# More query blocks beside the layer, a depthwise chunk moved to VectorE, and maxima spread by transposes one step after their fold

## The chip, the core and the metric

The kernel runs on one core of a Trainium2 chip. The metric is the device time of one execution in microseconds (us). The kernel before takes 5365.54 us, the median of three runs (5365.16 to 5367.03). All data are fp32.

## What is computed

The input x has four images of 64 x 64 tokens with 256 channels. Two layers follow each other.

```python
# layer 0: a gated block of scan and depthwise convolution, then a feed-forward
xz = layernorm(x) @ in_proj_W                 # 256 -> 2 * 384
x_proj, z = xz[..., :384], xz[..., 384:]
y_ssm = 0.5 * (scan_fwd(windows2x2(x_proj)) + scan_bwd(windows2x2(x_proj)))   # 8 states, 4 steps
y_dw = depthwise_conv3x3(x_proj)
y_conv = gelu(y_dw @ pw_W)
alpha = sigmoid(gate)
y = alpha * y_ssm + (1 - alpha) * y_conv
x1 = x + (y * silu(z)) @ out_W
x1 = x1 + gelu(layernorm(x1) @ fuse_W1 + b1) @ fuse_W2 + b2
# layer 1: attention over the 4096 tokens of each image
f, g, h = x1 @ Wf + bf, x1 @ Wg + bg, x1 @ Wh + bh     # 32, 32 and 256 wide
out = gamma * (softmax(g @ f.T) @ h @ Wo + bo) + x1
```

Both layers must give all their values; the output is `out`, of the shape of x.

## The kernel before, in words

**The first layer** goes in 32 layer blocks of 512 tokens (eight image rows), eight to an image. `first_layer` (L734) is a Python generator: each piece of it issues some instructions and then yields a number, its cost. For every layer block it runs `scan` (L413), which goes through 8 states times 3 time steps in both directions, in 48 scan steps: TensorE turns a decay tile into a PSUM bank (`turned`, L449), VectorE multiplies it with the state (`decayed`, L457 and L461), adds to the output (`given`, L467) and makes the next state (`carried`, L476). Between these pieces, `side` (L703) is fed in by credit (SHARE, 1.2): the depthwise convolution `conv` (L588) of the block before, its gate, its `tail` (L602) and the next block's `head` (L302). After the scan, `merge` (L547) turns the scan's output back to channels and adds it to xc, the projected input.

`depthwise` (L558) works on three chunks of 128 channels. Its argument `dense` says how many go over TensorE, as nine matmuls with diagonal weights (L565) and a copy on ACT (L571); each other chunk is nine operations on VectorE, L580 for the first tap and L582 for eight more. On the first image `dense` is 2, on the others 1. `tail` multiplies by pw_W (L613), takes Gelu on ACT (L618), scales by 1 - alpha on ACT (L625), adds alpha/2 times the merged scan on VectorE (L628), multiplies by the gate (L631), and goes on through out_W (L638), the feed-forward (L658, L669) and the values and keys of layer 1, which are written to memory.

**The attention** starts when the first image has left layer 0. An *early query block* is 128 queries of one image against its 4096 tokens. `weights` (L819) is a generator that makes the exponentials of the next block: scores on TensorE (L832), copies on ACT (L840), their maximum over tokens on VectorE (L846, L848, folded at L851), which is then made one number per query and spread over the partitions: two transposes (L854), a reduction (L856), a broadcast copy (L858), a matmul with the identity (L860), a copy on ACT (L862). Then for each of four tiles VectorE adds the negative maximum (L866) and ACT takes the exponential (L867). `attend` (L1013) multiplies the exponentials of the present block with the values (L1027), in eight steps of four value matmuls (512 tokens) each; after each step it takes one piece of `weights` of the next block and then calls `fill(RATE)` (L872), which takes pieces of the first layer until their costs make up RATE, 7.2. So RATE sets how much of the layer is issued beside one query block. `until` (L882) holds a new image's attention back until its layer blocks are done.

When the layer has ended, the rest of the attention goes by *late query blocks* of 256 queries (`late_weights` L912, `attend_late` L991), with the value matmuls on L1005 and the same spreading of maxima over L947 to L961.

**The order of work.** Every engine runs its instructions in one order, which the program's order of issue sets, with a scheduler that may move an instruction of a later piece ahead where the priorities allow it. TensorE's PSUM has three banks for the scan (`bank`), four for everything aside (`aside`, q0 to q3), and one for an accumulator (`pso`). SyncE's queue carries the loads of values (`vt`), queries, rests and the results.

The lines that pace the two are these:

```python
        for k in range(NI):
...
            next(beside, None)
            fill(RATE)
```

Of the kernel before, what the change touches and what calls it, by code (L numbers as in the profile page):

```python
# [22 lines left out]
AF = mybir.ActivationFunctionType  # L23
ALU = mybir.AluOpType
# [4 lines left out]
P = 128  # L29
# [11 lines left out]
CK = DIM // 8  # L41
EPS = 1e-5
SHARE = 1.2
RATE = 7.2


_VECS = [
# [12 lines left out]
def block_then_attention_kernel(  # L60
# [486 lines left out]
    def merge(at):  # L547

        y = merged.pop(at)
        xc = heads[at][1]  # L550
        for f in range(KI):
            py = bank()
            for t in range(4):
                nc.tensor.transpose(py[:, t * P : (t + 1) * P], y[:, t, f * P : (f + 1) * P], ident)
            nc.vector.scalar_tensor_tensor(xc[:, f, :], xc[:, f, :], dsum[:, f : f + 1], py, ALU.mult, ALU.add)
            yield 1.1

    def depthwise(ydw, dense):  # L558

# [28 lines left out]
    def conv(at):  # L588
        b = at // NBLK
        ydw = one.tile([P, KI, TOK], F32, tag="ff", name="ydw")  # L590
        ydws[at] = ydw
        yield from depthwise(ydw, KI - 1 if b == 0 else 1)

    def next_head(at):

# [6 lines left out]
    def tail(at):  # L602
# [7 lines left out]
        for f in range(KI):  # L610
# [10 lines left out]
                    AF.Gelu,  # L621
                )
            yield 2.58
        for f in range(KI):
            nc.scalar.activation(yz[:, f, :], yz[:, f, :], AF.Copy, scale=one_a[:, f : f + 1])  # L625

        for f in range(KI):
            nc.vector.scalar_tensor_tensor(  # L628
                yz[:, f, :], s[:, f, :], half_a[:, f : f + 1], yz[:, f, :], ALU.mult, ALU.add
            )  # L630
            nc.vector.tensor_tensor(yz[:, f, :], yz[:, f, :], zs[:, f, :], ALU.mult)  # L631
            yield 1.3
# [186 lines left out]
    def weights(b, q, es):  # L819


        fQ, gq = quarters[b], gqs.pop((b, q))
        mx = one.tile([P, TOK], F32, tag="mx", name="mx")
        for g in range(2):
            pr = four()

            with tc.high_priority():
                last = None
                for s in range(4):
                    at = g * TOK + s * P  # L830
                    for r in range(4):
                        ins = nc.tensor.matmul(  # L832
                            pr[r][:, s * P : (s + 1) * P], lhsT=fQ[CK * r : CK * (r + 1), at : at + P],
                            rhs=gq[CK * r : CK * (r + 1), :], start=True, stop=True,
                        )
                        last = behind(ins, last)
            for a in range(2):
                e = ep.tile([P, 2, TOK], F32, tag="eq", name="eq")
                for j in range(2):
                    nc.scalar.copy(e[:, j, :], pr[2 * a + j])  # L840
                es.append(e)
            yield
            for r in range(4):
                e = es[2 * g + r // 2]
                if g == 0 and r == 0:
                    nc.vector.tensor_tensor(mx, e[:, 0, :], e[:, 1, :], ALU.max)  # L846
                elif g == 1 or r > 1:
                    nc.vector.tensor_tensor(mx, mx, e[:, r % 2, :], ALU.max)  # L848
            if g == 0:
                yield  # L850
        nc.vector.tensor_tensor(mx[:, :QB], mx[:, :QB], mx[:, QB:], ALU.max)  # L851
        pm = aside()
        for c in range(2):
            nc.tensor.transpose(pm[:, c * P : (c + 1) * P], mx[:, c * P : (c + 1) * P], ident)  # L854
        nm = st.tile([P, 1], F32, tag="nm", name="nm")
        nc.vector.tensor_reduce(nm, pm[:, :QB], AX.X, ALU.max, negate=True)  # L856
        nmb = two.tile([P, P], F32, tag="nb", name="nmb")
        nc.vector.tensor_copy(nmb, nm.to_broadcast([P, P]))  # L858
        pn = aside()
        nc.tensor.matmul(pn[:, :P], lhsT=nmb, rhs=ident, start=True, stop=True)  # L860
        nb = two.tile([P, P], F32, tag="nb", name="nb")
        nc.scalar.copy(nb, pn[:, :P])  # L862
        yield
        for n, e in enumerate(es):
            e8 = e.rearrange("p r (s q) -> p (r s) q", s=4)
            nc.vector.tensor_tensor(e8, e8, nb.unsqueeze(1).broadcast_to([P, 8, P]), ALU.add)  # L866
            nc.scalar.activation(e, e, AF.Exp)  # L867
            yield
# [43 lines left out]
    def late_weights(b, q, odd, es):  # L912


        if b not in quarters:
            quarter(b, one, "norm" if b % 2 else "xo")
        fQ, gq = quarters[b], gqs.pop((b, q))
        mx = two.tile([P, 2, QB], F32, tag="uT", name="mx")
        for g in range(4):
            pr = four()  # L920
            for s in range(2):
                at = (g // 2) * TOK + (2 * (g % 2) + s) * P
                for r in range(4):
                    nc.tensor.matmul(  # L924
                        pr[r][:, s * QB : (s + 1) * QB], lhsT=fQ[CK * r : CK * (r + 1), at : at + P],
                        rhs=gq[CK * r : CK * (r + 1), :], start=True, stop=True,
                    )
            for a in range(2):
                pool, tag = SLOTS[8 * odd + 2 * g + a]
                e = pool.tile([P, 2, 2, QB], F32, tag=tag, name="eT")  # L930
                for j in range(2):
                    nc.scalar.copy(e[:, j], pr[2 * a + j].rearrange("p (s q) -> p s q", s=2))  # L932
                if g == 0 and a == 0:
                    nc.vector.tensor_tensor(mx, e[:, 0], e[:, 1], ALU.max)
                else:
                    for j in range(2):
                        nc.vector.tensor_tensor(mx, mx, e[:, j], ALU.max)  # L937
                es.append(e)
                yield
        yield  # L940
        yield
        both = one.tile([P, 2, QB], F32, tag="mx", name="m2")
        m2, nb = both[:, 0, :], both[:, 1, :]
        nc.vector.tensor_tensor(m2, mx[:, 0, :], mx[:, 1, :], ALU.max)
        pm = aside()
        for c in range(2):
            nc.tensor.transpose(pm[:, c * P : (c + 1) * P], m2[:, c * P : (c + 1) * P], ident)  # L947
        nm = st.tile([P, 2], F32, tag="nm", name="nm")
        nc.vector.tensor_reduce(
            nm, pm[:, :QB].rearrange("p (c k) -> p c k", c=2), AX.X, ALU.max, negate=True  # L950
        )
        wide = three.tile([P, 2, P], F32, tag="p", name="nmb")
        for c in range(2):
            nc.vector.tensor_copy(wide[:, c, :], nm[:, c : c + 1].to_broadcast([P, P]))
        yield
        pn = aside()
        for c in range(2):
            nc.tensor.matmul(
                pn[:, c * P : (c + 1) * P], lhsT=wide[:, c, :], rhs=ident, start=True, stop=True
            )  # L960
        nc.scalar.copy(nb, pn[:, :QB])  # L961
        for n, e in enumerate(es):
            e4 = e.rearrange("p r s q -> p (r s) q")
            nc.vector.tensor_tensor(e4, e4, nb.unsqueeze(1).broadcast_to([P, 4, QB]), ALU.add)  # L964
            nc.scalar.activation(e, e, AF.Exp)
            if n % 2:
                yield
# [42 lines left out]
                next(beside, None)  # L1010
        outcome(b, 2 * q, res, sums)

    def attend(b, q, es, beside, following):  # L1013

        res = load_rest(b, q, two, "res", 1)
        acc = pso.tile([P, TOK], F32, tag="pso", name="acc")
        for k in range(NI):
            for h in range(2):
                n = 2 * k + h
                if n + 4 < 2 * NI:  # L1020
                    load_values(b, q, n + 4)
                else:
                    following(n + 4 - 2 * NI)
                vt = vts.pop((b, q, n))
                for s in range(2):
                    a = (2 * h + s) * P
                    nc.tensor.matmul(  # L1027
                        acc[:, : DIM + 1], lhsT=es[k // 2][:, k % 2, a : a + P], rhs=vt[:, s, :],
                        start=(n == 0 and s == 0), stop=(n == 2 * NI - 1 and s == 1),
                    )  # L1030
            next(beside, None)
            fill(RATE)
        outcome(b, q, res, [acc])
# [17 lines left out]
    for n in range(4):  # L1051
        load_values(0, 0, n)
    es = []
    for _ in weights(0, 0, es):
        fill(RATE)
    a = 0
    while True:
# [6 lines left out]
        if late:  # L1064
            n0 = (b1, q1 // 2)
            load_late_queries(*n0)
            beside = twice(late_weights(*n0, 0, ahead))
            attend(b, q, es, beside, lambda n: load_late_values(*n0, n))
            es = ahead
            break  # L1070
        if q1 == 0:
            quarter(b1, one, "fQ")
        load_queries(b1, q1)
        attend(b, q, es, weights(b1, q1, ahead), lambda n: load_values(b1, q1, n))
        es = ahead
        a += 1
    odd, block = 0, n0
    while block:
# [98 lines left out]
```

## Time and profile before

| | value |
|---|---|
| median of three runs | 5365.54 us |
| the profiled execution, its time | 5371.37 us |
| its span, first to last instruction | 5369.6 us |
| mean granted TensorE clock | 0.978 |
| TensorE busy over the span | 5029.3 us (94%) |
| VectorE busy | 4558.3 us (85%) |
| ScalarE (ACT) busy | 3599.4 us (67%) |
| early query blocks (128 queries) | 76 |
| late query blocks (256 queries) | 26 |
| layer blocks | 32, of which 23 scans lie beside attention |

A row of a group reads: line, engine, operation, output <- inputs, size, count, then busy time in us and the mean duration of one in ns, then the idle time of the engine ahead of it and who ended it. A row of the chain of waits or the timeline reads: start in us, length in us, engine, line, tile, count. PE is TensorE's matmuls, PEld its weight loads, DVE VectorE, ACT ScalarE, POOL GpSimd, SP SyncE. A matmul of fp32 appears as two records.

The page's slices show the stages: the DMA row stands at 0 to 1 tenths while only the layer runs, at 3 while attention runs beside it, and at 5 in late attention.

### The profile page before, as it was taken

What the parts mean: (1) busy time and instruction counts of PE and PEld (TensorE: products, weight loads), DVE (VectorE), ACT (ScalarE), POOL (GpSimd) and SP (SyncE); (2) the same over time, 40 slices, a digit from 0 to 9 for tenths busy, and PEclk for the clock granted to TensorE, in tenths of its full rate; (3) what the DMA queues carried; (4) which work ended last, traced back from release to release, by engine and by line L of the source; (5) the groups of instructions that cost most, each with busy time, mean ns of one, the idle gap of its engine ahead of it and who ended that gap; (6) DMA issues with size and microseconds to landing.
All of it is one profiled execution on the core that took longest, in us unless ns stands there. A gap on an engine that the chain in (4) does not pass through costs nothing. (4 is left out here: it accounts for less than half of the span.)

```text
span 5369.6 us, 77772 instructions
## 1 busy us (share of the span) xinstructions
PE 5029.3 (94%) x27476; PEld 3585.9 (67%) x27476; DVE 4558.3 (85%) x8386; ACT 3599.4 (67%) x5530; POOL 206.0 (4%) x304
## 2 busy tenths in 40 slices
PE   7999999999999999999999999999999999999999
PEld 4555555666666666666666666666666667888887
DVE  7999999889988899889889998888998875666665
ACT  5767767778777677767777766767777744555554
POOL 0000000000000000000000000000000000000000
PEclk8999999999999999999999999999999999999999
DMA  1001001333333333333333333333343335555554
GB/s 47 26 30 31 19 25 31 98 109 107 115 113 112 114 112 114 118 115 107 111 116 111 115 116 107 114 114 113 102 123 113 110 116 165 146 146 146 146 146 138
DMA packets 333126, 558.45 MB, mean 104 GB/s; under 512 B 51904, under 2 KB 86976, under 8 KB 332736
## 3 DMA queue, kind: packets, MB, share of 16 engines
q1 hardware_dynamic: 330160, 551.52, 35.1%
q8 instruction: 217, 3.56, 0.3%
q10 hardware_dynamic: 2576, 1.97, 0.1%
q14 instruction: 173, 1.42, 0.1%
HBM read 494.49 MB, written 58.79 MB: 103 GB/s over the span
## 5 line engine op out<-in xcount | busy, mean ns | idle before, releaser
L1027 PE MATMUL acc<-vt,eq 128*128 128x257 f32 x4864 | 1234.2, 389 | 16.9 <-DVE res L975 13.0
L392 ACT ACTIVATE e<-dt,a_sc 128x384 f32<-128x384 f32 x1536 | 852.7, 611 | 347.0 <-PE bank L449 318.9
L1027 PEld LDWEIGHTS acc<-vt,eq 128*128 128x128 f32 x4864 | 891.1, 193 | 249.2 <-issue 116.6
L467 DVE SCALAR_TENSOR_TENSOR y<-p,bc,y 128x384 f32<-128x384 f32 x1536 | 948.8, 618 | 0.7
L449 PEld LDWEIGHTS bank<-ident,e 128*128 128x128 f32 x4320 | 524.3, 143 | 302.1 <-issue 125.7
L449 PE MATMUL bank<-ident,e 128*128 128x128 f32 x4320 | 647.8, 280 | 72.2 <-DVE p L461 29.3
L1005 PE MATMUL bank<-vt,eT 128*128 128x257 f32 x2496 | 625.8, 382 | 0.0
L476 DVE SCALAR_TENSOR_TENSOR h<-u,bc,p 128x384 f32<-128x384 f32 x1024 | 618.2, 621 | 0.1
L461 DVE TENSOR_TENSOR p<-bank,h 128x384 f32<-128x384 f32 x960 | 517.0, 552 | 52.4 <-PE bank L449 50.4
L1005 PEld LDWEIGHTS bank<-vt,eT 128*128 128x128 f32 x2496 | 467.1, 190 | 81.0 <-issue 12.9
L840 ACT COPY eq<-q 128x512 f32<-128x512 f32 x608 | 310.8, 593 | 179.7 <-PE q L832 166.4
L866 DVE TENSOR_TENSOR eq<-eq,nb 128x1024 f32<-128x1024 f32 x304 | 367.7, 1231 | 19.2 <-ACT nb L862 18.9
L867 ACT ACTIVATE eq<-eq 128x1024 f32<-128x1024 f32 x304 | 317.5, 1054 | 92.7 <-DVE eq L866 88.7
L937 DVE TENSOR_TENSOR mx<-mx,eT 128x512 f32<-128x512 f32 x364 | 252.0, 692 | 143.0 <-ACT eT L932 113.2
L848 DVE TENSOR_TENSOR mx<-mx,eq 128x512 f32<-128x512 f32 x456 | 317.0, 695 | 50.5 <-ACT eq L840 38.5
L932 ACT COPY eT<-q 128x512 f32<-128x512 f32 x416 | 213.2, 597 | 188.5 <-PE q L924 188.5
L392 ACT ACT_TABLE_LOAD x254 | 325.9, 1283 | 11.0 <-PE bank L449 6.8
L457 DVE SCALAR_TENSOR_TENSOR p<-bank,bc,u 128x384 f32<-128x384 f32 x480 | 294.1, 613 | 45.8 <-PE bank L449 45.6
L582 DVE SCALAR_TENSOR_TENSOR ydw<-xp,vec,ydw 128x512 f32<-128x512 f32 x448 | 325.4, 750 | 2.2
L613 PE MATMUL q<-ydw,wpw 128*128 128x512 f32 x576 | 269.3, 599 | 18.8 <-ACT eq L840 18.8
L964 DVE TENSOR_TENSOR eT<-eT,m 128x1024 f32<-128x1024 f32 x208 | 238.5, 1221 | 46.6 <-ACT m L961 46.6
L565 PE MATMUL q<-xp,dw 128*128 128x512 f32 x576 | 274.0, 597 | 2.4 <-ACT eq L840 2.4
(151 smaller groups left out, 7394.7 us busy)
## 6 DMA issues: line engine op xcount, KB each, us to landing
vt<-vod SPq DMA_DIRECT2D x1632, 257.0 KB, 2.8
vod<-vst SPq DMA_DIRECT2D x32, 514.0 KB, 4.4
xo<-in_x_dram SPq DMA_DIRECT2D x256, 64.0 KB, 2.7
xt<-in_x_dram SPq DMA_DIRECT2D x256, 64.0 KB, 1.9
x1d<-xo SPq DMA_DIRECT2D x32, 512.0 KB, 2.9
res<-x1d SPq DMA_DIRECT2D x76, 128.0 KB, 2.6
out_dram<-res SPq DMA_DIRECT2D x304, 32.0 KB, 1.6
fgd<-fg SPq DMA_DIRECT2D x32, 256.0 KB, 2.0
```

The lines of the kernel that those rows point to most:

```text
L392: nc.scalar.activation(e[:, f, :], dts[d][:, f, lo : lo + 3 * P], AF.Exp, scale=a_sc[:, d, f * NST + n : f * NST + n + 1],)
L449: nc.tensor.transpose(pa[:, f * P : (f + 1) * P], es[d, n][:, f, off : off + P], ident)
L461: nc.vector.tensor_tensor(p, pa[:, :INNER], hs[d], ALU.mult)
L467: nc.vector.scalar_tensor_tensor(y[:, t, :], p, bc[:, t, d, NST + n : NST + n + 1], y[:, t, :], ALU.mult, ALU.add)
L476: nc.vector.scalar_tensor_tensor(hs[d], u[d][:, t, :], bc[:, t, d, n : n + 1], p, ALU.mult, ALU.add)
L582: nc.vector.scalar_tensor_tensor(o, x_tap, w_tap, o, ALU.mult, ALU.add)
L840: nc.scalar.copy(e[:, j, :], pr[2 * a + j])
L848: nc.vector.tensor_tensor(mx, mx, e[:, r % 2, :], ALU.max)
L866: nc.vector.tensor_tensor(e8, e8, nb.unsqueeze(1).broadcast_to([P, 8, P]), ALU.add)
L867: nc.scalar.activation(e, e, AF.Exp)
L1005: nc.tensor.matmul(sums[c][:, : DIM + 1], lhsT=e[:, r % 2, s, c * P : (c + 1) * P], rhs=vt[:, s, :], start=(n == 0 and s == 0), stop=(n == ...
L1027: nc.tensor.matmul(acc[:, : DIM + 1], lhsT=es[k // 2][:, k % 2, a : a + P], rhs=vt[:, s, :], start=(n == 0 and s == 0), stop=(n == 2 * NI ...
```

## The change

Six edits. RATE goes from 7.2 to 5.7, so less of the layer is issued beside each step of a query block. On images after the first, `dense` goes from 1 to 0: all three depthwise chunks are on VectorE. In `weights` a yield is put between the fold (L851) and the transposes of the maxima, which makes nine pieces of it for eight steps; the generator of the present block is handed to `attend` as `own`, which takes its ninth piece in the first step. The spread of the maxima, early and late, is a transpose in place of a matmul with the identity. The scale alpha/2 is put on the merged scan by ACT at the end of `merge`, and in the tail VectorE applies 1 - alpha in its own operation, in place of the ACT scaling by 1 - alpha.

```diff
-RATE = 7.2
+RATE = 5.7
...
             nc.vector.scalar_tensor_tensor(xc[:, f, :], xc[:, f, :], dsum[:, f : f + 1], py, ALU.mult, ALU.add)
             yield 1.1
+        for f in range(KI):
+            nc.scalar.activation(xc[:, f, :], xc[:, f, :], AF.Copy, scale=half_a[:, f : f + 1])
...
-        yield from depthwise(ydw, KI - 1 if b == 0 else 1)
+        yield from depthwise(ydw, KI - 1 if b == 0 else 0)
...
-        for f in range(KI):
-            nc.scalar.activation(yz[:, f, :], yz[:, f, :], AF.Copy, scale=one_a[:, f : f + 1])
         for f in range(KI):
             nc.vector.scalar_tensor_tensor(
-                yz[:, f, :], s[:, f, :], half_a[:, f : f + 1], yz[:, f, :], ALU.mult, ALU.add
+                yz[:, f, :], yz[:, f, :], one_a[:, f : f + 1], s[:, f, :], ALU.mult, ALU.add
             )
...
         nc.vector.tensor_tensor(mx[:, :QB], mx[:, :QB], mx[:, QB:], ALU.max)
+        yield
         pm = aside()
...
-        nc.tensor.matmul(pn[:, :P], lhsT=nmb, rhs=ident, start=True, stop=True)
+        nc.tensor.transpose(pn[:, :P], nmb, ident)
...
         for c in range(2):
-            nc.tensor.matmul(
-                pn[:, c * P : (c + 1) * P], lhsT=wide[:, c, :], rhs=ident, start=True, stop=True
-            )
+            nc.tensor.transpose(pn[:, c * P : (c + 1) * P], wide[:, c, :], ident)
...
-    def attend(b, q, es, beside, following):
+    def attend(b, q, es, own, beside, following):
...
+            next(own, None)
             next(beside, None)
             fill(RATE)
...
-        attend(b, q, es, weights(b1, q1, ahead), lambda n: load_values(b1, q1, n))
-        es = ahead
+        beside = weights(b1, q1, ahead)
+        attend(b, q, es, own, beside, lambda n: load_values(b1, q1, n))
+        es, own = ahead, beside
```

More of the change, by code (lines that the diff above doesn't have):

```diff
@@ L1053, in block_then_attention_kernel @@
     es = []
-    for _ in weights(0, 0, es):
+    own = weights(0, 0, es)
+    for _ in own:
         fill(RATE)
@@ L1067, in block_then_attention_kernel @@
             beside = twice(late_weights(*n0, 0, ahead))
-            attend(b, q, es, beside, lambda n: load_late_values(*n0, n))
+            attend(b, q, es, own, beside, lambda n: load_late_values(*n0, n))
             es = ahead
```

## The prediction

> **What bounds the kernel now.** I read the busy time by stretch first, because the three stages have different limits. Stage A (0 to 912 us) is the layer alone on the first image, stage B (to 4492) the layer with early query blocks beside it, stage C late attention alone. Columns: length, then busy time of PE, PEld, DVE, ACT, POOL, with instruction counts; granted clock; DMA share; GB/s.
>
> ```profile
> 0.00:912.00 912.00, 822.84 (x3443) 511.53 (x3443) 840.44 (x1714) 644.42 (x1039) 55.78 (x87) 0.94 0.10 30
> 912.00:4492.00 3580.00, 3335.84 (x18959) 2361.26 (x18959) 3164.99 (x5886) 2524.44 (x3859) 150.22 (x217) 0.98 0.39 113
> 4492.00:5369.60 877.60, 870.65 (x5080) 713.11 (x5078) 552.87 (x788) 430.52 (x633) 0.00 (x0) 1.00 0.50 144
> ```
>
> C is TensorE to 99%, with VectorE at 63%. In B both are nearly full (93% and 88%); neither alone explains the length. ACT (71%) and DMA (39%) are not the limit. The chain of waits gives C's price:
>
> ```profile
> 4379.19 8.04 PE q L613 x18
> ...
> 4548.77 7.14 PE bank L1005 x32
> ...
> 4615.82 7.14 PE bank L1005 x32
> ```
>
> The same piece returns after 67.05 us, which is two late blocks of 256 queries: 33.5 us each. The L613 piece prices 18 records of 128x512 at 8.04 us. Then the waits of B (total us, times, longest):
>
> ```profile
> PE q L854 <- DVE mx L851: 37.5, 31, 3.2
> ...
> PE q L860 <- DVE nmb L858: 5.5, 7, 2.0
> ```
> ```profile
> DVE xo L673 <- PE q L669: 55.8, 33, 11.8
> DVE p L461 <- PE bank L449: 50.1, 51, 4.7
> ```
>
> Each engine waits for the other, in small pieces: the scan's transposes (L449) feed VectorE (L457, L461) through three PSUM banks, so one cannot run far ahead. Last the groups and, for prices, VectorE's timeline:
>
> ```profile
> L1027 PE MATMUL acc<-vt,eq 128*128 128x257 f32 x4864 | 1234.2, 389 | 16.9 <-DVE res L975 13.0 <-issue 2.7 <-PE bank L449 0.6
> ...
> L866 DVE TENSOR_TENSOR eq<-eq,nb 128x1024 f32<-128x1024 f32 x304 | 367.7, 1231 | 19.2 <-ACT nb L862 18.9
> ...
> L582 DVE SCALAR_TENSOR_TENSOR ydw<-xp,vec,ydw 128x512 f32<-128x512 f32 x448 | 325.4, 750 | 2.2
> ...
> L565 PE MATMUL q<-xp,dw 128*128 128x512 f32 x576 | 274.0, 597 | 2.4 <-ACT eq L840 2.4
> ```
> ```profile
> 2529.74 0.61 DVE L467 SCALAR_TENSOR_TENSOR y<-p,bc,y 128x384 f32<-128x384 f32 x1
> 2530.27 1.14 DVE L476 SCALAR_TENSOR_TENSOR h<-u,bc,p 128x384 f32<-128x384 f32 x2
> 2531.33 0.61 DVE L467 SCALAR_TENSOR_TENSOR y<-p,bc,y 128x384 f32<-128x384 f32 x1
> ```
>
> A 0.61 us instruction starts 0.53 after the one before it: neighbours overlap by some 0.08 us. So I price VectorE by the spacing of starts, read the same way for each form: tap 0.665 (first tap 0.395), 128x512 maximum 0.605, exponent's add 1.14.
>
> **What the Trainium skill says.** In "Perfetto Trace Analysis", the section "Identifying the Most-Contended Engine" takes occupancy as a fair measure for VectorE but not matmul busy time for TensorE; here modelled ends overlap (389 ns mean against 229 per record in the chain, 3.67 us for 16), so TensorE is also priced by spacing. The same page, "Transposes", wants a logical transpose issued as one: the trace shows two records for each ordinary fp32 matmul (L860: 152 for 76 query blocks) and one for each transpose (L854: 152 for 2 x 76). "VectorE: DVE Perf Modes", "The perf-mode tier table", has fp32 two-tensor operations at 1x only; its errata section's (N+151)/0.96 gives 691 ns at 512, and L848 has 695. "ScalarE: Activation LUTs", "What ACT_TABLE_LOAD costs": 1283 ns; every load here is 1283. The drain it adds cannot be seen here.
>
> **The change, by parts.** The compiled instruction order of both kernels gives the counts: 94 early query blocks for 76, and 17 late blocks of 256 for 26.
>
> *Stage C.* Nine late blocks go: 9 x 33.5 = 302. Each remaining one spreads its maxima with two transposes for two matmuls, two records of 0.14 us less on the bound engine: 17 x 0.28 = 5. C: **-307**.
>
> *Eighteen more query blocks in B.* TensorE each: 64 records x 0.229 = 14.7, scores 2 x 1.17 (32 records in 1.17 on the timeline) = 2.3, three transposes 0.4: 17.4, in all +314. VectorE each: 4 x 1.14 + 7 x 0.605 + 1.3 (fold, reduction, copy, outcome) = 10.1, in all +181. ACT (310.8 + 317.5 + 19.9)/76 = 8.5 each (L840, L867, L862), +153, less 42 table loads x 1.28 = 54: about 70% of a longer B, still cover. DMA: 144 more value loads of 257 KB, plus their queries, rests and results on SP's queue; the rate goes to about 130 GB/s, under the 144 that C already carries with 8 us of waits. Nothing.
>
> *Depthwise chunk to VectorE.* Per layer block TensorE loses 18 records, 8.04 us (24 x = -193), and an ACT copy; VectorE gains 8 x 0.665 + 0.395 = 5.7 (+137). L613 then waits for VectorE's last tap instead of a matmul; behind it in TensorE's queue stand value matmuls and scan transposes. Before, such a wait was 1 us in total. Its price is in the rivals.
>
> *Maxima.* The fold and the transposes are now a step apart (some 4.9 us: B over 94 x 8 steps). Behind the waiting transposes stood the whole TensorE queue; the 37.5 and 5.5 us go, and a record of 0.14 per block. What is late next is the fourth add and exponential, issued in the next block's first step and needed six steps on; it sits ahead of that block's score copies on ACT by 1.05 us. Bounds: -53 (43 us scaled by 94/76) to +20 (a fifth of the 94 exponentials exposed). I take **-20**, as about half of a TensorE wait shows in the time (below).
>
> *Scaling.* Three ACT copies of 0.72 us move from between Gelu and VectorE's L628 to the end of the merge. L628 waited 9.8 us for them in B; there they now wait for L555 ahead of score copies and exponentials. Bounds: -10 to +50 (2 us in each of 24 layer blocks, were ACT late); ACT is idle 29%. I take 0.
>
> *Sum in B.* TensorE +314 - 193 - 11 (second record of 76 spreads) = +110; VectorE +181 + 137 = +318. How does that become time? I cut the trace of before from its first to its last scan step in B (3417 us) into pieces of 12 scan steps, and set each piece's length beside the work that the instruction order puts in it, at the prices above (TensorE 3253, VectorE 3004 in all). A fit gives length = 0.53 TensorE + 0.56 VectorE, scatter 2.2 us on a mean of 37; pieces of 8 or 16 give nearly the same. So neither engine is covered by the other: each us of either costs about half. On stage A, where VectorE is the longer as it nearly will be in B, the rule gives 0.53 x 791 + 0.56 x 820 = 878 for 867 measured, 1.3% too much. For B: 0.53 x 110 + 0.56 x 318 = 236; half of A's error on 3417 is 22. **+214**.
>
> Total: +214 - 20 - 307 = -113. The profiled execution took 5371.4 (span 5369.6), so 5258; the median of the runs, 5365.5, is 5.8 lower, so **5253**.
>
> **Rivals.**
> *The engines slide past each other, as in A.* There the length was 867 over a busier engine of 820, 1.057. In B the busier becomes 3253 + 110 = 3363; x 1.057 = 3555, +138. With -20 and -307: -189, **5176**. For it: A has the same balance of both engines and no worse waits. Against: A has no query blocks with their maximum chain.
>
> *The quarters of a layer block do not even out; slower.* In the new order a layer block is four query blocks in fixed phase. Work per quarter, TensorE/VectorE: 26.9/32.6, 32.0/34.6, 42.3/30.0, 47.7/48.6. The longer of each sums to 158.1, against 144.3 before (25.5/25.3, 31.1/32.6, 37.5/28.4, 48.7/45.5), where 149.9 was measured: 1.039 times. Then 164.3, +14.4 a layer block, 23 of them: +331. The place is the quarter with the taps, where TensorE stands at L613 and the scan's transposes for VectorE, and the next, heavy in tail matmuls, where VectorE stands; the maxima then bring nothing. +331 - 307 = +24: **5390**. It decides from 307/23 = 13.3 us a layer block. For it: the three banks. Against: on A the same sum of longer parts comes out above the measured length (882 for 867), so pieces this long do even out somewhat.
>
> *A wash.* B grows by 296 to 317 and the time stays within 0.2%, 10.7 us, about what a measurement of this kernel can tell from no change. It needs the fit's rise plus the upper bounds of maxima and scaling. That the change does not move the blocks is excluded by the counts.
>
> **How the numbers follow.** Forecast 0.53 (own range 5205 to 5310); sliding 0.20; between forecast and a wash, still faster, 0.07; wash 0.06; quarters 0.14. Faster 0.80, same 0.06, slower 0.14. The range runs from below the sliding case, 5140 (the maxima at their better bound), to the quarters' 5395.
>
> **What would show it.** C near 571 us with 33.2 to 33.5 per late block; B near 3775; VectorE's busy time in B near 3480 and above 90%, TensorE's near 3445; waits for L851 near nothing. A layer block of some 158 to 159 us for 149.9. I am wrong if B's growth passes 307, which new waits of TensorE for taps or of VectorE for scan banks would show, or stays under 150 with VectorE near 95%.

## The result and the profile after

The changed kernel takes 5325.56 us (median of four, 5322.37 to 5326.12), the kernel before 5366.28: a ratio of 0.9923, 95% interval 0.9906 to 0.9940. It is faster by 41 us, where 113 were forecast: inside the stated range of 5140 to 5395 and in the direction forecast, but little more than a third of the size. The profiled execution took 5325.51 us with a span of 5323.7.

The busy time by stretch, for the three stages of the changed kernel (length, then PE, PEld, DVE, ACT, POOL; clock; DMA share; GB/s):

```profile
0.00:890.00 890.00, 810.90 (x3436) 501.44 (x3436) 835.35 (x1713) 642.94 (x1039) 54.11 (x87) 0.96 0.10 31
890.00:4752.00 3862.00, 3524.82 (x20802) 2563.98 (x20803) 3465.13 (x6391) 2603.01 (x4027) 155.15 (x217) 0.96 0.43 126
4752.00:5323.70 571.70, 565.45 (x3274) 461.71 (x3272) 358.67 (x510) 278.86 (x408) 0.00 (x0) 1.00 0.50 144
```

C is 572 us, as forecast (571). Its chain repeats every 66.60 us, 33.3 for a late block:

```profile
4875.03 7.14 PE bank L1004 x32
...
4941.63 7.14 PE bank L1004 x32
```

B is too long: 3862 where 3775 was forecast. To compare kernels I cut at events that all have: A is up to the first scan step of the tenth layer block, B from there to the last scan step (23 layer blocks), then the tail to the first late value matmul, then C. Lengths in us:

| kernel | A | B | tail | C | span |
|---|---|---|---|---|---|
| before | 944.8 | 3416.7 | 131.4 | 876.7 | 5369.6 |
| changed | 919.5 | 3704.3 | 130.8 | 569.1 | 5323.7 |
| difference | -25 | +288 | -1 | -308 | -46 |

So two terms are off: A gained 25 where nothing was forecast, and B grew by 288 where +194 was. The waits of B at the scan's banks in the kernel before, two of TensorE's and one of VectorE's, then TensorE's and VectorE's waits in the changed one (us in total, times, longest):

```profile
PE bank L449 <- DVE p L457: 17.8, 13, 2.4
PE bank L449 <- DVE p L461: 15.6, 12, 2.9
```
```profile
DVE p L457 <- PE bank L449: 37.0, 32, 3.1
```

```profile
PE bank L449 <- DVE p L461: 60.6, 49, 4.7
PE bank L449 <- DVE p L457: 29.6, 26, 3.2
...
PE q L861 <- DVE nmb L859: 17.6, 17, 3.0
PE q L855 <- DVE mx L851: 17.5, 12, 2.7
```
```profile
DVE xo L673 <- PE q L669: 80.4, 32, 8.3
DVE mx L846 <- ACT eq L840: 57.0, 22, 9.2
...
DVE p L461 <- PE bank L449: 39.8, 36, 2.4
...
DVE p L457 <- PE bank L449: 19.7, 13, 4.3
```

The wait for the fold (L851) halved, from 37.5 to 17.5, and did not vanish; 12 us of it came back one link on, at the spread's transpose (L861, 5.5 before). The large new wait is the scan's transposes standing for VectorE's L457 and L461: 90 us, 33 before. And the granted clock of B fell, from 0.98 to 0.96. One such place of the changed kernel, TensorE's timeline, then the same microseconds as windows (columns as above; the last but two is the clock):

```profile
2721.63 0.55 PE L449 MATMUL bank<-ident,e 128*128 128x128 f32 x3 [3.19 <-DVE p L461]
2722.29 2.07 PE L615 MATMUL q<-ydw,wpw 128*128 128x512 f32 x2
```
```profile
2720.00:2724.00 4.00, 2.25 (x5) 1.04 (x6) 4.00 (x8) 1.81 (x3) 0.00 (x0) 0.76 0.00 0
2724.00:2728.00 4.00, 2.57 (x32) 2.01 (x34) 4.00 (x9) 3.53 (x5) 0.00 (x0) 0.50 0.07 20
2728.00:2732.00 4.00, 4.00 (x20) 2.98 (x17) 4.00 (x8) 2.69 (x5) 0.00 (x0) 0.50 0.27 66
```

VectorE is busy in all of these 12 us, with taps and exponents' additions between the scan's operations. TensorE stands 3.19 us for it, and afterwards runs at half clock. The Trainium skill describes that in "TensorE: Matmul & The Clock Gate", "What's actually happening": the gate opens with recent activity and closes to one half without it. The 0.50 after the gap agrees. The record of the granted clock holds only full and half, so B's mean of 0.964 (0.985 before) means 7.3% of the time at half clock (270 us) for 3.1%.

### The profile page after: what moved, and what is told of

It reads as the page before. It is cut to its first block, busy times and chain, and to the rows that moved or that the text cites. A ratio compares the mean times of both kernels' runs of the same rounds, so it can differ in the third digit from the quotient of the medians.

```text
span 5323.7 us, 78254 instructions
## 1 busy us (share of the span) xinstructions
PE 4901.2 (92%) x27510; PEld 3527.1 (66%) x27510; DVE 4659.1 (88%) x8611; ACT 3524.8 (66%) x5473; POOL 209.3 (4%) x304
## 4 chain that ended last, share of the span: by engine, by line
PE 32%; DVE 15%; ACT 7%; issue 2%; DMA 1%; POOL 0%; SPq 0%; DVEq 0%; ACTq 0%; POOLq 0%
PE acc L1026 8%; PE bank L1004 7%; PE acc L1004 2%; DVE ydw L584 2%; PE q L669 2%; DVE eq L867 2%; DVE y L467 2%; PE bank L449 2%; PE q L658 2%; ACT eq L840 2%; DVE h L476 2%; DVE mx L848 2%; DVE p L461 1%; PE q L925 1%; PE q L615 1%
## 5 line engine op out<-in xcount | busy, mean ns | idle before, releaser
L1026 PE MATMUL acc<-vt,eq 128*128 128x257 f32 x6016 | 1542.6, 394 | 20.2 <-issue 8.8
L1026 PEld LDWEIGHTS acc<-vt,eq 128*128 128x128 f32 x6016 | 1122.0, 196 | 309.4 <-issue 136.2
L461 DVE TENSOR_TENSOR p<-bank,h 128x384 f32<-128x384 f32 x960 | 512.1, 547 | 40.5 <-PE bank L449 40.1
L867 DVE TENSOR_TENSOR eq<-eq,nb 128x1024 f32<-128x1024 f32 x376 | 453.0, 1220 | 11.7 <-ACT nb L863 10.8
L584 DVE SCALAR_TENSOR_TENSOR ydw<-xp,vec,ydw 128x512 f32<-128x512 f32 x640 | 462.7, 741 | 0.2
L1004 PE MATMUL bank<-vt,eT 128*128 128x257 f32 x1600 | 404.6, 382 | 0.0
L1004 PEld LDWEIGHTS bank<-vt,eT 128*128 128x128 f32 x1600 | 299.1, 189 | 52.5 <-issue 9.0
L457 DVE SCALAR_TENSOR_TENSOR p<-bank,bc,u 128x384 f32<-128x384 f32 x480 | 291.5, 607 | 21.6 <-PE bank L449 21.2
L832 PE MATMUL q<-gq,fQ 32*128 32x128 f32 x6016 | 252.0, 293 | 43.4 <-ACT eq L840 17.3
L832 PEld LDWEIGHTS q<-gq,fQ 32*128 32x128 f32 x6016 | 207.4, 194 | 117.2 <-ACT eq L840 27.1
L658 PE MATMUL q<-h2T,wf 128*128 128x512 f32 x512 | 245.4, 611 | 11.0 <-ACT eq L840 9.7
L938 DVE TENSOR_TENSOR mx<-mx,eT 128x512 f32<-128x512 f32 x238 | 164.7, 692 | 91.7 <-ACT eT L933 72.1
```

What stands on the lines that cost most here:

```text
L461: nc.vector.tensor_tensor(p, pa[:, :INNER], hs[d], ALU.mult)
L584: nc.vector.scalar_tensor_tensor(o, x_tap, w_tap, o, ALU.mult, ALU.add)
L832: ins = nc.tensor.matmul(pr[r][:, s * P : (s + 1) * P], lhsT=fQ[CK * r : CK * (r + 1), at : at + P], rhs=gq[CK * r : CK * (r + 1), :], sta ...
L1004: nc.tensor.matmul(sums[c][:, : DIM + 1], lhsT=e[:, r % 2, s, c * P : (c + 1) * P], rhs=vt[:, s, :], start=(n == 0 and s == 0), stop=(n == ...
L1026: nc.tensor.matmul(acc[:, : DIM + 1], lhsT=es[k // 2][:, k % 2, a : a + P], rhs=vt[:, s, :], start=(n == 0 and s == 0), stop=(n == 2 * NI ...
```

## The experiments

Two theories stood at first. *Clock*: B grew more than forecast because TensorE, standing for VectorE, runs slowly afterwards. *Phase*: taps and tail matmuls lie in different parts of a layer block and do not even out, as the slower rival of the prediction said. Ratios are to the kernel before on the same chip, with 95% intervals; stage lengths are from each run's profile. "Work" is the instruction order's count at the prediction's prices, over B.

One caution for every length of B below. The cut at the last scan step doesn't always leave the same query blocks on either side. Counted by their value matmuls, B holds 72 query blocks in the kernel before and 90 in the changed one, but 91 in `rate_only` and `no_dense` and 71 in `dense_only` and `filler_chunk`; the tail has the rest. Where the counts differ, B and tail together are the fairer measure, and are given too.

**The four parts alone**, each put on the kernel before.

```diff
-RATE = 7.2
+RATE = 5.7
```

> The kernel before with RATE 5.7 alone: 94 early query blocks and 17 late ones, the depthwise chunk still on TensorE. Theory 'clock' (the part of stage B's growth that the forecast missed is TensorE at a lower granted clock, because it stands idle for VectorE): here TensorE is the longer engine (3587 us of work beside 3197), it seldom stands, so the clock in B stays at 0.98 or above; the fit's rule gives +286 in B and C gives -302: about 5350. Rival 'phase' (the four query blocks of a layer block do not even out, whatever the clock): the longer of the two engines over pieces of 12 scan steps sums to 3576 for 3294 before, times 1.031 is +291: 5355, with no fall of the clock. Both expect about the same time; it is the base for the chunk's part.

Measured 5406.75, ratio 1.0066 (1.0051 to 1.0081): slower. A 949, B 3772.9, tail 112, C 574. B grew by 356 and not by 286 to 291; the clock stayed (0.984). B holds 19 more query blocks here, one of them out of the tail, and the rule's 286 is for the work of these 19. So the rule under the forecast's largest term was short by 70 in a kernel where TensorE did not slow down: the clock is not its cause.

```diff
-        yield from depthwise(ydw, KI - 1 if b == 0 else 1)
+        yield from depthwise(ydw, KI - 1 if b == 0 else 0)
```

> The kernel before with all three depthwise chunks of the later images on VectorE, nothing else: 74 early query blocks and 27 late ones. Work between the first and last scan step in B: TensorE 3061, VectorE 3127 us (before: 3253 and 3004). The fit's rule: -32 in B, +33.5 for one more late block: 5367. Theory 'clock': VectorE is now the longer engine, TensorE stands for it, and the granted clock in B falls from 0.985 to about 0.965, which adds some 60: 5425. Rival 'phase': longer pieces sum to 3336 for 3294, +43, and +33.5: 5443, with the clock as before.

Measured 5428.16, ratio 1.0105 (1.0088 to 1.0122): slower. B 3455.1, +38, although TensorE has 192 us less to do. The tail is 16 shorter with one query block fewer, and C 31 longer with one late block more: 55 in the span. The clock fell to 0.948. The time and the clock's direction speak for the theory of the clock, but not yet for the clock as the cause.

The maxima's edits alone (the yield, `own`, the transposes):

```diff
         nc.vector.tensor_tensor(mx[:, :QB], mx[:, :QB], mx[:, QB:], ALU.max)
+        yield
...
-        nc.tensor.matmul(pn[:, :P], lhsT=nmb, rhs=ident, start=True, stop=True)
+        nc.tensor.transpose(pn[:, :P], nmb, ident)
...
+            next(own, None)
             next(beside, None)
```

> The kernel before with the maxima alone: a step between fold and transposes, the ninth piece taken in the next block's first step, transposes in place of matmuls with the identity, early and late. 74 early blocks and 27 late ones, so C gets 33.5 longer less 8 for the transposes, and B two query blocks shorter (-8 by the fit). The forecast put the step at -20: then 5364. If the step brings nothing: 5384. If TensorE's waits for the fold (43 us) come off the time in full: 5341.

Measured 5346.56, ratio 0.9953 (0.9938 to 0.9968). B 3406.6 (-10), tail 89.7, C 903.7. The ratio is 25 us, the number of the last case, but the account is another: the two early blocks that went had lain in the tail (-42) and are now one late block, about even, so the +25 that all three cases had for it was not paid. What remains is -10 in B, some -7 in C (0.25 us a late block) and some -7 in the tail: near the -20 and -5 of the forecast.

The scaling's edits alone:

```diff
+            nc.scalar.activation(xc[:, f, :], xc[:, f, :], AF.Copy, scale=half_a[:, f : f + 1])
...
-            nc.scalar.activation(yz[:, f, :], yz[:, f, :], AF.Copy, scale=one_a[:, f : f + 1])
...
-                yz[:, f, :], s[:, f, :], half_a[:, f : f + 1], yz[:, f, :], ALU.mult, ALU.add
+                yz[:, f, :], yz[:, f, :], one_a[:, f : f + 1], s[:, f, :], ALU.mult, ALU.add
```

> The kernel before with the scaling alone: alpha/2 on the merged scan at the end of merge, 1 - alpha in VectorE's operation, no ACT scaling behind Gelu. The forecast put it at 0. The trace of the changed kernel shows stage A's layer blocks at 96.5 us for 101, and only this edit touches stage A: then A gets 21 to 25 shorter and the time is 5343 if B gains nothing, and about 5265 if each of the 23 layer blocks in B gains the same 4.4. If stage A's gain came from a chance shift of the order of work instead, nothing: 5366.

Measured 5336.93, ratio 0.9934 (0.9919 to 0.9949). A 925.9 (-19), B 3406.7 (-10). The layer block in A fell from 100.65 to 96.53 us, in this kernel and in every other with this edit and the same costs of the pieces. Four layer blocks of A, 340 to 740 us, in the kernel before and then in the changed one: the busy times (columns as above), then VectorE's waits.

```profile
340.00:740.00 400.00, 374.80 (x1572) 231.57 (x1572) 379.30 (x760) 292.17 (x469) 24.58 (x36) 0.95 0.09 26
```
```profile
340.00:740.00 400.00, 382.64 (x1640) 234.27 (x1639) 392.67 (x793) 302.25 (x488) 24.06 (x37) 0.99 0.08 26
```

```profile
DVE xo L642 <- PE q L638: 6.9, 4, 2.3
DVE p L457 <- PE bank L449: 6.7, 10, 0.9
DVE h L275 <- POOL rstd L273: 5.0, 4, 1.2
DVE xo L673 <- PE pa L449: 0.5, 1, 0.5
```
```profile
DVE h L275 <- POOL rstd L273: 4.1, 4, 1.0
DVE vst L697 <- PE q L693: 1.9, 4, 0.5
```

VectorE is the limit there (95% busy before, 98% after). Of four layer blocks' 19 us of waits 13 go: the tail's L642, which stood at the end of the chain Gelu, ACT scaling (1.93 us for three), L628, L638, no longer waits, nor does the scan. The trace of `scale_only` has the same two waits left as the changed kernel, so it is this edit. Nothing was taken off VectorE; a link was taken out of a chain that it had to wait for. The idle 29% of ACT, on which the forecast rested, did not hide that link.

**The pairs and the parts undone.**

> The kernel before with the maxima and the scaling, RATE 7.2 and the chunk on TensorE left. Alone they gave ratios of 0.9953 and 0.9934; if they add up, 0.9887 of before, about 5306, and this beats the changed kernel (5325), so that RATE and the chunk together cost some 20. If the two share one gain: 0.993 to 0.995, 5330 to 5340.

Both edits of the two helpful parts, RATE 7.2 and one chunk on TensorE. Measured 5297.57, ratio 0.9872 (0.9858 to 0.9887), A 922.7, B 3380.7, tail 88, C 902. They add up, and this beats both kernels: put on top of it, RATE and the chunk together cost 28 us.

> RATE 5.7 and the chunk on VectorE alone, on the kernel before, without maxima and scaling. Alone RATE cost 40 and the chunk 60 (ratios 1.0066 and 1.0105 of before). Theory 'phase': longer pieces of 8 scan steps for this order come to 160.3 a layer block or less, B +14.9 x 23 = 343 at most, C -302: up to 5407. If maxima and scaling bring here what they bring on the kernel before (70 together), the changed kernel's 5325 means 5395. If the parts simply added: 5466.

RATE and the chunk without the other two. Measured 5369.42, ratio 0.9993 (0.9984 to 1.0001): neither faster nor slower. B 3723.9, 49 less than with RATE alone; 40 less with the tail, since about one query block is in the tail here that is in B there. Maxima and scaling bring 44 us of span on top of this pair, not 70: 29 in A, 20 in B, 5 in C, less 10 more in the tail.

```diff
-        yield from depthwise(ydw, KI - 1 if b == 0 else 0)
+        yield from depthwise(ydw, KI - 1 if b == 0 else 1)
```

> The changed kernel with one chunk of the later images back on TensorE: 94 early blocks, TensorE 3569 us of work between the scan steps, VectorE 3195. Theory 'clock': the clock comes back to 0.98 and each us of TensorE's work costs 1.05 (3417 over 3253 before, 3773 over 3587 with RATE alone): B's scan part 3748 for 3704, so 5325 + 44 = 5369. Rule of the forecast (0.53 TensorE + 0.56 VectorE): +28, 5353. Rival 'phase': longer pieces 3585 for 3587, no change, 5325.

This undoes the chunk in the changed kernel. Measured 5344.87, ratio 0.9961 (0.9947 to 0.9975); B 3738.8, clock 0.982. So here the chunk on VectorE gains 35 in B. But the tail is 109.4 here and 130.8 in the changed kernel, with up to one query block more: B and tail together gain 13, the span 18. The forecast gave the chunk -102 for TensorE and +77 for VectorE, -25; alone on the kernel before it cost 38 in B and 55 in the span. The sign depends on RATE.

```diff
-        yield from depthwise(ydw, KI - 1 if b == 0 else 0)
+        yield from depthwise(ydw, KI - 1 if b == 0 else at % 2)
```

> The changed kernel with one chunk back on TensorE in every second layer block of the later images. Work: TensorE 3470, VectorE 3265. Theory 'clock': if the loss grows with the time that TensorE stands, it is convex and the middle lies below the mean of the two ends (5325 and no_dense): TensorE's 3470 at 1.05 is 3644, 60 less than the 3704 of the changed kernel, to be met only if the clock is back at 0.98; with half of the clock's fall (36) left, 5300. Rival 'phase': longer pieces 3585, as both ends: 5325.

Measured 5305.76, ratio 0.9888 (0.9873 to 0.9903); B 3699.9. The first half of the move gains 39 in B, the second loses 4; with the tail (115.5) the first gains 33 and the second loses 20. So the middle is better than either end, which fits a cost that rises with imbalance, and the whole move is past the optimum.

```diff
         nc.vector.tensor_tensor(mx[:, :QB], mx[:, :QB], mx[:, QB:], ALU.max)
-        yield
...
-            next(own, None)
             next(beside, None)
```

> The changed kernel without the step between fold and transposes (and without the piece left for the next block), the transposes kept. The forecast put the step at -20: 5345. If TensorE's whole wait for the fold (43 us, times 94/76) was on the path: 5378. If the step brings nothing since VectorE is the limit where the fold lies: 5325.

Measured 5327.48, ratio 0.9919 (0.9904 to 0.9933): the step brings nothing in the changed kernel (B is 12 longer without it, the tail 10 shorter).

**Is the slow clock a cost?** Matmuls of constants, whose result nobody reads, beside the taps:

```diff
+            if dense == 0:
+                spare = aside()
             o = ydw[:, f, :].rearrange("p (r c) -> p r c", r=ROWS)
...
                 if tap % 3 == 2:
+                    if dense == 0:
+                        for _ in range(1):
+                            nc.tensor.matmul(spare[:, :512], lhsT=ident, rhs=wpw.rearrange("p k f -> p (k f)")[:, :512], start=True, stop=True)
                     yield 2.0
```

> The changed kernel with nine more matmuls of 128x512 per layer block on the later images, of constants, whose result nobody reads, one beside each three taps of the depthwise convolution: TensorE gets back as much work as the chunk was (3559 for 3379), while VectorE keeps all its taps. It leaves the output as it is. Theory 'clock': the filler lies where TensorE stood and ran at half clock (over the first third of a layer block the clock was 0.89 to 0.97): the clock rises to about 0.98, the idle time of some 129 us there is filled and the 72 us of slower records come back, so 180 us of added work cost nothing or less: 5300 to 5325. If the lower clock is only a by-product and costs nothing: 180 less the 129 of idle time filled, 5375. If TensorE's idle time cannot be filled either: 5505.

Measured 5370.95, ratio 1.0008 (1.0000 to 1.0017); B 3752.7. The clock came back to 0.982 and the time did not: the clock's theory missed by 46 and more, and the number of the case where the low clock is a mere by-product (5375) was met within 4. Of 180 us of added work B took in 132.

> The changed kernel with nine matmuls of 128x128 of constants per layer block on the later images, whose result nobody reads, one beside each three taps (in 'filler9' they were 128x512). The output stays as it is. Work added to TensorE: 51 us between the scan steps. If TensorE's half-clock time (269 us in B, which makes its records 66 to 72 us longer) costs the stage, and a little work is enough to hold the clock: the clock rises towards 0.975 and B falls, 5290 to 5315. If TensorE's idle and slow time is slack behind VectorE: B takes the 51 in, 5320 to 5330, whatever the clock does. If the waits at the aside banks that the filler takes in turn cost: 5345 and more.

The same with 128 columns: 5322.30, ratio 0.9898 (0.9883 to 0.9912); B 3701.6 for 3704.3, the clock 0.973. 51 us of work, and the 46 us that these matmuls stood for the aside banks that they take, cost nothing, and a clock 0.01 higher gave nothing that can be told.

> The kernel 'dense_only' (RATE 7.2, all taps of the later images on VectorE, clock in B 0.947, 360 us at half clock) with nine matmuls of 128x512 of constants per layer block, whose result nobody reads. The output stays as it is. TensorE's work goes from 3061 back to 3231, VectorE's stays at 3127. If the low clock costs time: B falls below 'dense_only''s 3455 although TensorE has 170 us more, total under 5428. If idle and slow time is slack behind VectorE: B takes most of the 170 in (of 180 in 'filler9' it took 132), 5428 to 5470. If TensorE's work has its full price here too: 5600.

On `dense_only`: 5432.43, ratio 1.0101 (1.0086 to 1.0116). B, `dense_only` and then with the filler:

```profile
945.90:4401.00 3455.10, 3094.66 (x17597) 2221.71 (x17597) 3162.47 (x5898) 2366.71 (x3659) 150.82 (x210) 0.95 0.37 110
```
```profile
946.90:4409.70 3462.80, 3189.94 (x18047) 2258.68 (x18045) 3165.39 (x5901) 2365.12 (x3654) 151.12 (x210) 0.98 0.36 110
```

TensorE has 170 us more to do, the clock returns from 0.948 to 0.978, its busy time grows by only 95, and the length by 8. So TensorE's standing and half-clock time are for the most part slack behind VectorE: raising the clock shortened B in none of the three. A gain from the clock that the filler's own work takes back just then cannot be told from no gain. As the cause of the largest part of the forecast's miss the clock is out in any case, by `rate_only`.

**Is it the phase?** Two kernels with the same instructions in another order: a group of taps yields 3.0 for 2.0, and the tail's pieces 0.8 of theirs.

```diff
-                    yield 2.0
+                    yield 3.0
...
-            yield 2.58
+            yield 2.06
...
-        yield from weave(tail(at - 1), 46.0, next_head(at), 14.0)
+        yield from weave(tail(at - 1), 36.8, next_head(at), 14.0)
```

> The kernel 'half' with other costs for the same pieces: a group of three taps yields 3.0 for 2.0 and the tail's pieces 0.8 of theirs, so that the taps lie over more scan steps and the tail's matmuls later. No instruction is added or taken away: TensorE 3463 and VectorE 3255 us of work between the scan steps, as in 'half' (3470, 3265). Theory 'phase': the longer engine over pieces of 8 scan steps sums to 156.7 us a layer block for 158.8, so B gets 23 x 2.1 = 48 shorter: 5258. Rule of the forecast (0.53 TensorE + 0.56 VectorE): -9, 5297. Theory 'clock': the amounts are the same, so the idle times are, 5306.

Measured 5398.70, ratio 1.0048 (1.0031 to 1.0065): 93 slower than `half`, where phase said 48 faster. A is 33 longer (99.98 us a layer block, since the costs also pace the first image), the tail 16, and B 46 longer, at 3745.5.

> The kernel 'no_dense' with other costs for the same pieces: a group of three taps yields 3.0 for 2.0, the tail's pieces 0.8 of theirs. TensorE 3546, VectorE 3187 us of work (3569, 3195 in 'no_dense'). Theory 'phase': longer pieces of 8 scan steps sum to 155.8 us a layer block for 158.3, 23 x 2.5 = 57 shorter: 5288. Rule of the forecast: -17, 5328. Price of 1.05 for each us of the longer engine: -24, 5321.

Measured 5371.89, ratio 0.9997 (0.9988 to 1.0005). A 28 longer, tail 27 longer, B 3713.8: 25 shorter, where phase said 57 and the price by TensorE's work 24. But B holds 1.4 query blocks fewer than `no_dense` (89.6 for 91) and the tail so many more; B and tail together are 2 longer, so the other order gained nothing. So the sums of the longer engine over pieces do not foretell what another order does. The theory of the phase in that form falls too. What in the order made `spread_half` 46 longer in B stays open.

**The price of a query block in the other direction**, RATE 9.0 on `maxima_scale`:

```diff
-RATE = 7.2
+RATE = 9.0
```

> The kernel 'maxima_scale' with RATE 9.0 for 7.2: 60 early query blocks for 74 and 34 late blocks for 27. Theory 'full price' (in B TensorE is full, a query block costs there what it takes on TensorE at 1.05 and more: RATE alone put 356 us on B for 18 blocks, 19.8 each, where C pays 16.8): each block moved back to C gains 3.0, 14 of them 42: 5256. Rule of the forecast (0.53 TensorE + 0.56 VectorE on 2985 and 2855 for 3238 and 3002): -216 in B and +234 in C, 5316. No change: 5298.

Measured 5327.48, ratio 0.9912 (0.9896 to 0.9929): slower than `maxima_scale` (0.9872), by 28 us of span. B fell by 221, close to the fit's 216; C rose by 235 and the tail by 15. B and tail together fell by 206 for 14 query blocks, 14.7 each. The new price of 19.8 was wrong here. It was also too high upwards, since the 356 held 19 query blocks: B and tail together rose by 337 for 18, 18.7 each, and from `maxima_scale` to `no_dense` by 379 for 20, 19.0 each.

## Why the prediction was wrong, point by point

**C, -307.** Right: -308, with 33.3 us for a late block.

**The sum in B is where it failed**, in the rule "length = 0.53 TensorE + 0.56 VectorE" put on the additional query blocks. For the nineteen that B took with RATE alone the rule gives 286 (0.53 x 334 + 0.56 x 193; the prediction had 268 for its eighteen), and B grew by 356. On the kernel with maxima and scaling the same step (`no_dense` against `maxima_scale`) gives 284 by the rule and 358 in B. The windows of B for the kernel before and the one with RATE alone:

```profile
944.80:4361.50 3416.70, 3185.05 (x18144) 2257.48 (x18142) 3056.33 (x5706) 2442.63 (x3733) 145.92 (x210) 0.98 0.38 113
```
```profile
949.00:4721.90 3772.90, 3521.04 (x20651) 2549.85 (x20649) 3274.17 (x6011) 2591.44 (x3973) 149.19 (x210) 0.98 0.43 125
```

TensorE's share is 93.3%, as it was before (3185 of 3417, 93.2%), while VectorE's idle time grew from 360 to 499 us: the length went up with TensorE's busy time (x 1.105 and x 1.104), and VectorE's 193 us of work fit beside it. Read so, a us of TensorE cost 1.07, not 0.53 with a share for VectorE. In the six kernels with a chunk on TensorE whose work was counted, B is 1.04 to 1.06 times TensorE's work (3381 over 3238 and 3417 over 3253 at RATE 7.2; 3739 over 3569, 3773 over 3587 and 3714 over 3546 at 5.7; 3159 over 2985 at 9.0). With all taps on VectorE, where the two have nearly equal work, it is not: 3455 over 3061, 1.13, in `dense_only`, and 3704 over 3379, 1.10, in the changed kernel. Downwards, with RATE 9.0, TensorE's 253 us less gave 221, 0.87 each, and there the rule held. The rule is a local slope, read from pieces of 12 scan steps of one kernel, and was carried 18 query blocks to the side where TensorE's work leads more clearly. There "neither engine is covered by the other" was too strong. Why the slope is lower downwards stays open.

**The correction by stage A, -22,** went the wrong way: A, where VectorE is the limit, says nothing of what TensorE's work costs when TensorE is the limit.

**The chunk, -25** (0.53 x -193 + 0.56 x 137): right in sign on RATE 5.7 (-35 in B with maxima and scaling, -49 without; -13 and -40 with the tail), but not because each us of either engine costs half. At each RATE there is a kernel with the chunk on TensorE, one with the taps on VectorE, and one with the taps and about as much work for TensorE whose result nobody reads. B in us, then B and tail together:

| | chunk on TensorE | taps, and filler on TensorE | taps alone |
|---|---|---|---|
| RATE 7.2 (before, filler_chunk, dense_only) | 3416.7, 3548.1 | 3462.8, 3572.7 | 3455.1, 3570.7 |
| RATE 5.7 (no_dense, filler9, changed) | 3738.8, 3848.2 | 3752.7, 3880.3 | 3704.3, 3835.1 |

The relief of TensorE, the last column against the middle one, gives 8 at 7.2 and 48 at 5.7 (2 and 45 with the tail), at equal numbers of query blocks. So TensorE's work had nearly no price where VectorE has as much to do, and about a quarter of its full price (48 of 180) where TensorE has more. What the taps cost, the middle against the first, is less sure: 46 in B at 7.2, though with one query block fewer, and 14 in B or 32 with the tail at 5.7. (The filler is not the chunk itself: it reads constants, waits for no data, and takes aside banks in turn.)

**The maxima, -20,** and 5 in C: about right on the kernel before; in the changed kernel the step alone gives nothing measurable. The forecast named the fourth add and exponential as late next; the value matmuls stood for them only 1.6 us in B of the changed kernel, and 12 us of the wait came back at the spread's transpose.

**The scaling, 0:** missed. It gives -19 to -29 in A and 10 in B. The bound of -10 counted L628's wait in B and not the end of the chain in A, which I had not looked at.

**Signs that the prediction named.** C, its late block and VectorE's 3465 us in B (90%) came as forecast; B's length, TensorE's busy time (3525 for 3445) and the wait for L851 did not. B's growth of 288 stayed below the 307 of the slower rival, which so failed its own test. Of the two waits that were to show it, TensorE's for taps came to 2.9 us, and VectorE's for the scan's banks fell from 87 to 60; what grew is TensorE's own wait at these banks for VectorE, 33 to 90, which the rival named as its place. Of the cases the wash, with 296 to 317, came nearest in B, and A's 25 us made a clear gain of it.

**In all,** taking the parts one after the other (RATE, then the chunk, then maxima and scaling), B grew by 356, -49 and -20: against the forecast the query blocks are 88 too dear, the chunk 24 too cheap, and the rest as said. These steps lead from one kernel to the other and so must add up to the 288; in another order the chunk's share is another. C is -308, A -25, the tail -1. That the total missed by 72 and not by more is luck in part: A's 25 came from a part that the forecast had put at nothing. RATE and the chunk, two of the four parts, cost 28 us together.

## What to carry to other kernels

A slope that is fitted to pieces of one profile holds near that profile; before it is carried to a quarter more query blocks, ask which engine's work will lead there, and compare it with that engine's work at full price. Where the two are nearly equal, neither price told the length here. Moving work from one stage to another gains only by what the stages price differently: here 128 queries cost 16.8 us in the late stage and beside the layer, B and tail together, 14.7 (from RATE 9.0 to 7.2) to 18.7 or 19.0 (from 7.2 to 5.7). A copy on an engine with idle time can still be a link in a chain that the limiting engine waits for.

## What was not expected of the hardware

In the place shown, TensorE's granted clock fell to one half after a stand of 3.19 us and stayed there for some 10 us. Its busy time and its share are inflated by such stretches: in `dense_only`, 170 us of added matmuls raised the clock from 0.948 to 0.978 and the busy time by only 95. Its busy share alone, 91% in the changed kernel and 93% before, did not tell on which side of the balance a kernel stands.
